# Four graph layers on 64 graphs: layer 2 projects before it aggregates

## The chip, the cores and the metric

The kernel runs on one core of one Trainium2 chip. A core has five engines with an instruction queue each: TensorE (PE in the profile; its weight loads are listed as PEld), VectorE (DVE), ScalarE (ACT), GpSimd (POOL) and SyncE (SP), which here issues all DMA transfers. The metric is the device time of one launch in microseconds; a time is the median of several runs. All data is fp32.

## What is computed

64 graphs of 256 nodes with 512 features go through four layers. Each layer normalizes x, clips it at zero to give h, computes a graph layer from h and the adjacency matrix, and adds the result to x. Layer 2, the one that the change is about, and layer 3 read:

```python
def _L2_gnn_ref(x, a, kernel):          # x is h, 256 x 512; a is 256 x 256
    t = jnp.einsum('bnm,bmf->bnf', a, x)
    out = jnp.einsum('bnf,fd->bnd', t, kernel)
    out = jax.nn.relu(out)
    mask = (jnp.sum((x != 0).astype(jnp.float32), axis=-1, keepdims=True) > 0).astype(jnp.float32)
    return out * mask

def _L3_gnn_ref(x, adj, W):
    deg = jnp.sum(adj, axis=-1, keepdims=True)
    agg = jnp.einsum('bij,bjf->bif', adj, x) / jnp.maximum(deg, EPS)
    cat = jnp.concatenate([x, agg], axis=2)
    out = jnp.einsum('bnf,of->bno', cat, W)
    return jax.nn.relu(out)

# layer l:  h = jnp.maximum(_layernorm(x, axis=-1), 0.0);  x = x + layer_l(h, adj, ...)
```

Layer 0 is an attention layer (a softmax over the nodes of `leaky_relu(Wh1 + Wh2)`, masked where the adjacency is at most 0.5, then `elu`). Layer 1 uses A + I scaled on both sides by the square root of its row sums, with a bias and a ReLU. A product A h W can be taken as (A h) W or as A (h W); the result is the same but for rounding.

## The kernel before

**Products of halves.** A product of two matrices is taken by 2 x 2 blocks with seven block products instead of eight (Winograd's form of Strassen's scheme). The left matrix is held as seven blocks A11, A12, S1, A22, S2, S4, S3 and the right one as B11, B21, B22, T1, T2, T3, T4N; S and T are sums and differences of blocks. `project` (L525) issues the seven products of one or more operand pairs into three PSUM banks, pz, pv and py. Between the four products in pz, the block there is copied out (`snap`, L555) by ACT or DVE; `add` (L561) adds the blocks in pv and py on DVE. The first three result blocks end in a tile c, or where `places` says; the last one stays in pz and is given to `last`. An operand is either `Weighted` (L488: a node tile times one of the five weight tiles wb, two matmuls to a product) or `Gathered` (L503: blocks of the adjacency aT and their sums aw times a projected tile y, one matmul to a product).

**A layer.** In layers 0, 1 and 2, `aggregate` (L464) first multiplies h by the adjacency (eight matmuls, L474, into two PSUM banks pt). This leaves the aggregate with the features along the partitions, as the projection needs it. `left_sums` (L450) copies it into the tile xw and makes S1 (L459); `more_sums` (L440) makes S2 on DVE and S3 and S4 on POOL (L446). Then `project` multiplies xw by the layer's weight, 14 matmuls, and `into_x` (L602) adds the result to xs on DVE, with the row sums (total) that the next norm needs. The first two graphs (`FIRST`) do layer 0 in another order.

Layer 3 already goes the other way. It turns h3 so that its features lie along the partitions: DVE transposes 32 x 32 blocks into the tile hb (L820), and 16 DMA transfers (L825) move the blocks to their place in hw, in runs of 128 bytes. DVE makes hw's S1 (L830), `more_sums` the rest. A first `project` (L840) multiplies hw by wb4 and leaves its blocks in the tiles y and y12 (the copies are L582 and L841, the totals L584); four differences (L848, three on DVE, one on POOL) complete y. Four sums of blocks of aT (L854 to L860, on POOL) make aw. A second `project` (L863) takes hw times wb3 and aT times y together, three matmuls to a product. Before that, aT is scaled in place by the row 1 / degree (L814), which `along` (L361) turns and spreads with a DVE transpose and two DMA transfers.

Layer 1 uses A + I, made by three POOL operations (L745, L749) in the tile ahT.

**The order.** Every instruction is entered by `op` (L219) with its engine, a planned duration, what it reads and writes, and its tiles. `Plan.place` (L72) then simulates all engines and gives each the next instruction that can start, by urgency and due time; it also gives out the buffers of each tag. The planned durations are multiplied by `STRETCH`; a product on PE is ranked as if its input came `SPARE` us later. `APART` is the distance of the graphs' due times, shortened to a part `LATE` for the last `LAST` graphs. The engines then execute their lists strictly in that order. Buffers are given by tag (L879): among them xs (7), aT (6), h (3), xw (5, for xw0 to xw2, hw and y), mva (6, for e, ahT and aw), c (3), hb (1, also used while the weights are loaded, L267 and L326).

Of the kernel before, what the change touches and what calls it, by code (L numbers as in the profile page):

```python
# [11 lines left out]
ALU = mybir.AluOpType  # L12
AX = mybir.AxisListType

P = 128
Q = 32
# [3 lines left out]
ALPHA = 0.2  # L20
NEG_INF = -9000000000000000.0
HOP = 0.25
APART = 14.0
ON_PE = 3
FIRST = 2
LAST, LATE = 4, 0.3

STRETCH = {"DVE": 1.15, "ACT": 1.1, "POOL": 1.15, "PE": 1.0, "DMA": 1.0}
SPARE = 0.3

# [119 lines left out]
def kernel(  # L152
# [39 lines left out]
    class Tiles:  # L192
# [5 lines left out]
        def declare(self, name, shape, pool=None, tag=None):  # L198
            tag = pool or tag or name
            self.tiles[name] = Buffered(shape, tag, f"{name}_{self.name}")  # L200
# [63 lines left out]
    def weight(n, w):  # L264

        me = Tiles(f"w{n}", 0.0)
        me.declare("b12", [P, FH, OH], tag="hb")  # L267
        for at, i, j in ((B11, 0, 0), (None, 0, 1), (B22, 1, 1), (B21, 1, 0)):
            block = w[i * FH * P : (i + 1) * FH * P, j * OH : (j + 1) * OH].rearrange(
                "(k p) o -> p k o", p=P  # L270
            )
            me.op("DMA", 256, lambda g, at=at, block=block: nc.sync.dma_start(  # L272
                g["b12"] if at is None else wb[n][:, at], block),
                  (), ["b12" if at is None else f"=wb{n}.{at}"])
        weight_sums(me.op, n, "b12")
        if n == 0:
            logit_weights(me)
# [43 lines left out]
    def last_weight():  # L321

        me = Tiles("w3", 0.0)
        op, declare = me.op, me.declare
        for n in range(2):
            declare(f"b12_{n}", [P, FH, OH], tag="hb")  # L326
        for c in range(O // P):
            j, o = divmod(c * P, OH)
            declare(f"w3n{c}", [P, 2 * F], tag="h")
            op("DMA", 512, lambda g, c=c: nc.sync.dma_start(  # L330
                g[f"w3n{c}"], w3[c * P : (c + 1) * P, :]), (), [f"w3n{c}"])
            for n in range(2):
                for i in range(NC):
                    pw = f"pw{c}{n}{i}"
                    declare(pw, [P, FH, P], "ps")

                    def go(g, c=c, n=n, i=i, pw=pw):
                        for k in range(FH):
                            f0 = n * F + (i * FH + k) * P
                            nc.tensor.transpose(  # L340
                                g[pw][:, k], g[f"w3n{c}"][:, f0 : f0 + P], ident
                            )

                    op("PE", 0.23, go, [f"w3n{c}", "=ident"], [pw])
                    at = (B21 if i else B11) if j == 0 else (B22 if i else None)
                    key = f"b12_{n}" if at is None else f"=wb{3 + n}.{at}"
                    op("ACT", 0.38, lambda g, n=n, at=at, o=o, pw=pw: nc.scalar.copy(
                        (g[f"b12_{n}"] if at is None else wb[3 + n][:, at])[:, :, o : o + P],
                        g[pw]), [pw], [key])
        for n in range(2):  # L350
            weight_sums(op, 3 + n, f"b12_{n}")
# [4 lines left out]
    def graph(b):  # L356
# [251 lines left out]
               reads + to_keys, to_keys + ([f"{t}.{key}"] if sums else []), urgent=urgent)  # L608

        declare("ab", [P, NC, N], tag="ab")
        declare("aT", [P, NC, N])
# [121 lines left out]
        else:  # L735
# [7 lines left out]
        declare("ahT", [P, NC, N], tag="mva")  # L743
        flat = lambda t: t.rearrange("p c n -> p (c n)")
        op("POOL", 0.75, lambda g: nc.gpsimd.tensor_copy(  # L745
            flat(g["ahT"])[:, P : 3 * P], flat(g["aT"])[:, P : 3 * P]), ["aT"], ["ahT.off"])
        for c in range(NC):
            at = slice(3 * c * P, (3 * c + 1) * P)
            op("POOL", 0.5, lambda g, at=at: nc.gpsimd.tensor_tensor(  # L749
                flat(g["ahT"])[:, at], flat(g["aT"])[:, at], ident, ALU.add),  # L750
               ["aT", "=ident"], [f"ahT.{c}"])
        aggregate("h1", "ahT", 1, ["ahT.off", "ahT.0", "ahT.1"])

        def scaled(g, i, to, block, j):
# [36 lines left out]
           ["mask.0", "mask.1"], ["mask.0", "mask.1"])  # L791


        aggregate("h2", "aT", 2)

        def masked(i, key, y, y_keys, to, to_keys, n, at, tag):
            v = f"v2{tag}"
            declare(v, [P, n], tag=f"ex{n}")
            op("ACT", 0.5 if n == 256 else 0.72, lambda g: nc.scalar.activation(
                g[v], y(g), AF.Relu, scale=g["mask"][:, i : i + 1]), y_keys + [f"mask.{i}"], [v],  # L800
               urgent="pz2" in y_keys)
            into_x(2, key, at, 0.43 if n == 256 else 0.69,
                   lambda g, kw: nc.vector.scalar_tensor_tensor(
                       to(g), g[v], 0.0, to(g), ALU.add, ALU.add, **kw), [v], to_keys)

        first, second, third = pieces(2)
        project([Weighted("xw2", 2)], 2, plain_keep, 0.38, plain_total, lambda _: masked(*first, "a"))
        masked(*second, "b")
        masked(*third, "c")
        norm(3)  # L810


        along("pr", lambda g: g["rdeg"], ["rdeg"])
        op("DVE", 0.69, lambda g: nc.vector.tensor_tensor(  # L814
            g["aT"], g["aT"], g["pr"].rearrange("p (o n) -> p o n", o=1).to_broadcast([P, NC, N]),
            ALU.mult), ["pr", "aT"], ["aT"], urgent=True)

        declare("hb", [P, NC, F])
        for c in range(NC):
            op("DVE", 0.71, lambda g, c=c: nc.vector.transpose(g["hb"][:, c, :], g["h3"][:, c, :]),  # L820
               [f"h3.{c}"], [f"hb.{c}"])
        declare("hw", [P, 7, FH, P], tag="xw")
        parts = [(a, q) for a in range(P // Q) for q in range(P // Q)]
        for a, q in parts:
            op("DMA", 32, lambda g, a=a, q=q: nc.sync.dma_start(  # L825
                g["hw"][q * Q : (q + 1) * Q, : 2 * NC].rearrange("j s k n -> j (s k) n")[
                    :, :, a * Q : (a + 1) * Q],
                g["hb"][a * Q : (a + 1) * Q].rearrange("j c (k q r) -> q j (c k) r", q=P // Q, r=Q)[q]),
               ["hb.0", "hb.1"], [f"hw.{a}{q}"], holds=0.7)
        op("DVE", 0.43, lambda g: nc.vector.tensor_tensor(  # L830
            g["hw"][:, S1], g["hw"][:, S1], g["hw"][:, A22], ALU.add),
           [f"hw.{a}{q}" for a, q in parts], [f"hw.{i}" for i in (A11, A12, A22, S1)], urgent=True)
        more_sums("hw")

        declare("y", [P, 7, OH], tag="xw")
        declare("y12", [P, OH], tag="ex256")
        places = {(0, 0): (lambda g: g["y"][:, B11], f"y.{B11}"),
                  (0, 1): (lambda g: g["y12"], "y12"),
                  (1, 1): (lambda g: g["y"][:, B22], f"y.{B22}")}
        project([Weighted("hw", 4)], 4, plain_keep, 0.38, plain_total,  # L840
                lambda pz: op("ACT", 0.38, lambda g: nc.scalar.copy(g["y"][:, B21], g[pz]),  # L841
                              [pz], [f"y.{B21}"], urgent=True), places=places)
        for eng, us, to, i, j in (("DVE", 0.43, T1, None, B11), ("POOL", 0.85, T3, B22, None),
                                  ("DVE", 0.43, T2, B22, T1), ("DVE", 0.43, T4N, B21, T2)):
            name = lambda n: "y12" if n is None else f"y.{n}"
            of = lambda g, n: g["y12"] if n is None else g["y"][:, n]
            on = nc.vector if eng == "DVE" else nc.gpsimd
            op(eng, us, lambda g, on=on, to=to, i=i, j=j: on.tensor_tensor(  # L848
                g["y"][:, to], of(g, i), of(g, j), ALU.subtract), [name(i), name(j)],
               [f"y.{to}"], urgent=True)  # L850

        declare("aw", [P, 4, P], tag="mva")
        block = lambda g, c, i: g["aT"][:, c, i * P : (i + 1) * P]
        op("POOL", 0.5, lambda g: nc.gpsimd.tensor_tensor(  # L854
            g["aw"][:, 0], block(g, 0, 1), block(g, 1, 1), ALU.add), ["aT"], [f"aw.{S1}"])
        op("POOL", 0.5, lambda g: nc.gpsimd.tensor_tensor(
            g["aw"][:, 1], g["aw"][:, 0], block(g, 0, 0), ALU.subtract),
           ["aT", f"aw.{S1}"], [f"aw.{S2}"])
        for at, to, i in ((2, S3, 1), (3, S4, 0)):
            op("POOL", 0.5, lambda g, at=at, i=i: nc.gpsimd.tensor_tensor(  # L860
                g["aw"][:, at], block(g, 1, i), g["aw"][:, 1], ALU.subtract),
               ["aT", f"aw.{S2}"], [f"aw.{to}"])
        project([Weighted("hw", 3), Gathered("aT", "aw", "y")], 3, plain_keep, 0.38, plain_total,  # L863
                lambda _: relu_add(3, *pieces(3)[0]))
        _, second, third = pieces(3)
        relu_add(3, *second)
# [10 lines left out]
    for b in range(B):  # L877
        graph(b)
    buffers = dict(  # L879
        xs=7, a_nat=1, ab=1, aT=6, h=3, mva=6, xw=5, c=3, off=1, junk=1, ex256=2, ex512=2,  # L880
        a_rows=1, a_cols=1, turned=1, row=4, pl=1, pr=1, hb=1, ps=8,
    )
    for tag in ("stats", "total", "mv", "rstd", "nb", "deg", "dh", "rdeg", "lg", "top", "den", "mask"):
        buffers[tag] = 6
# [34 lines left out]
```

## Time and profile before

| | |
|---|---|
| median of 3 runs | 2832.87 us (2832.54 to 2833.22) |
| the profiled execution | 2832.82 us, of which 2831.0 us from the first to the last instruction (the span) |
| granted clock of TensorE | 1.000 |
| DMA | 159.10 MB in 493747 packets, 424644 of them under 512 bytes; 23.9% of the 16 DMA engines' time on SP's queue |
| largest group of DMA issues | hw<-hb, 1024 of 32.0 KB each (16 per graph), 609 ns median for SP to issue one |

An entry of the profile's groups reads: line, engine, operation, output <- inputs, shape, count | busy time in us, mean ns of one | idle time of the engine in front of them, and what ended it. Buffer numbers are left out of the names, so hw0 and hw1, or y and y12, are one name. An fp32 matmul appears as two MATMUL records and two LDWEIGHTS records. Records on PE overlap: the sum of their durations is more than the time in which PE was busy.

These are some of the times of one instruction that are used later:

```
L820 DVE STREAM_TRANSPOSE hb<-h 128x512 f32<-128x512 f32 x128 | 86.2, 689
L848 DVE TENSOR_TENSOR y<-y 128x256 f32<-128x256 f32 x128 | 79.9, 625
L848 DVE TENSOR_TENSOR y<-y,y 128x256 f32<-128x256 f32 x64 | 27.7, 433
L848 POOL TENSOR_TENSOR y<-y,y 128x256 f32<-128x256 f32 x64 | 61.6, 962
L454 ACT COPY xw<-pt 128x512 f32<-128x512 f32 x192 | 112.4, 585
L457 ACT COPY xw<-pt 128x256 f32<-128x256 f32 x192 | 71.4, 372
```

### The profile page before, as it was taken

The page shows a single profiled execution, that of the slowest core. Times are in us where ns is not written, and L with a number is a line of the kernel's source. Part 1 is how long each engine was busy: PE and PEld are TensorE (multiplying, and loading weights), DVE is VectorE, ACT ScalarE, POOL GpSimd, SP SyncE. Part 2 cuts the span into 40 slices and gives each one's busy share as a digit, 9 for nine tenths or more (in the row PEclk, how much of TensorE's full clock was granted, in tenths as well). Part 3 has the DMA queues.
Part 4 walks back from the last instruction along what each step waited for, and adds up shares of the span by engine and source line. Part 5 has one row for each costly group of instructions (what it writes and reads, how often), then busy time and mean ns, then how long its engine had stood idle before and what let it go on. Part 6 is the DMA issues. An engine that isn't in the chain of part 4 may idle for free.

```text
span 2831.0 us, 42966 instructions
## 1 busy us (share of the span) xinstructions
PE 2813.3 (99%) x12999; PEld 2464.8 (87%) x12999; DVE 1911.0 (68%) x5111; ACT 1707.6 (60%) x4118; POOL 1202.9 (42%) x2333
## 2 busy tenths in 40 slices
PE   8999999999999999999999999999999999999999
PEld 5888888888888888888888888888888888888888
DVE  7776667666666766667667666676666666666654
ACT  6766666666666666666656566666665666556552
POOL 7654434344344444443443434444434344343341
PEclk9999999999999999999999999999999999999999
DMA  5123222222222222222222222222222222221112
GB/s 173 25 64 74 67 48 56 63 47 59 57 49 64 49 55 63 46 59 51 55 64 49 55 62 47 59 52 53 65 45 58 55 46 52 42 52 39 43 33 53
DMA packets 493747, 159.10 MB, mean 56 GB/s; under 512 B 424644, under 2 KB 460108, under 8 KB 493516
## 3 DMA queue, kind: packets, MB, share of 16 engines
q1 hardware_dynamic: 493516, 156.36, 23.9%
q8 instruction: 104, 1.70, 0.3%
q14 instruction: 127, 1.04, 0.1%
HBM read 89.00 MB, written 33.68 MB: 43 GB/s over the span
## 4 chain that ended last, share of the span: by engine, by line
PE 98%; POOL 0%; DVE 0%; DMA 0%; ACT 0%; issue 0%; SPq 0%; DVEq 0%; POOLq 0%
PE pz L543 43%; PE pt L474 23%; PE pv L543 21%; PE py L543 11%; PE pwa_w L311 0%; POOL wb L260 0%; DMA a_rows_w<-in_L_gnn_a_dram 0%; PE po L723 0%; ACT h L436 0%; PE pw_w L302 0%; DMA pl<-dpl 0%; PE pt L705 0%; SPq L272 0%; DMA dpl<-tpl 0%; POOL xw L446 0%
## 5 line engine op out<-in xcount | busy, mean ns | idle before, releaser
L543 PE MATMUL pz<-wb,xw 128*128 128x256 f32 x3072 | 764.2, 379 | 3.5 <-ACT wh L582 2.1
L543 PEld LDWEIGHTS pz<-wb,xw 128*128 128x128 f32 x3072 | 582.9, 190 | 85.0 <-ACT wh L582 1.9
L543 PE MATMUL pz<-wb,hw 128*128 128x256 f32 x2048 | 524.2, 379 | 0.5 <-ACT c L582 0.5
L543 PEld LDWEIGHTS pz<-wb,hw 128*128 128x128 f32 x2048 | 389.0, 190 | 53.7 <-ACT c L582 0.9
L582 ACT COPY c<-pz 128x256 f32<-128x256 f32 x570 | 208.0, 370 | 329.7 <-PE pz L543 328.7
L436 ACT ACTIVATE h<-xs,nb,rstd 128x512 f32<-128x512 f32 x512 | 398.4, 809 | 10.3 <-POOL nb L433 7.2
L543 PE MATMUL pv<-wb,xw 128*128 128x256 f32 x1536 | 394.3, 379 | 0.9 <-DVE mv L401 0.8
L446 POOL TENSOR_TENSOR xw<-xw 128x256 f32<-128x256 f32 x384 | 299.6, 800 | 164.3 <-DVE xw L442 74.1
L543 PEld LDWEIGHTS pv<-wb,xw 128*128 128x128 f32 x1536 | 291.5, 190 | 41.2 <-POOL wb L260 0.9
L584 DVE TENSOR_TENSOR c<-pv,c 128x256 f32<-128x256 f32 x380 | 160.3, 422 | 232.6 <-PE pv L543 194.7
L415 ACT ACTIVATE h<-xs,mv 128x512 f32<-128x512 f32 x384 | 276.5, 721 | 6.2 <-POOL mv L412 4.9
L543 PE MATMUL pv<-wb,hw 128*128 128x256 f32 x1024 | 262.5, 379 | 0.0
L474 PE MATMUL pt<-ahT,h 128*128 128x256 f32 x1024 | 240.9, 379 | 0.9 <-ACT h L436 0.9
L474 PE MATMUL pt<-aT,h 128*128 128x256 f32 x1024 | 236.8, 379 | 0.0
L474 PE MATMUL pt<-e,h 128*128 128x256 f32 x992 | 225.0, 379 | 0.4 <-ACT e L675 0.4
L409 POOL TENSOR_SCALAR mv<-total 128x1 f32<-128x1 f32 x192 | 111.7, 582 | 261.2 <-DVE xs L691 134.0
L454 ACT COPY xw<-pt 128x512 f32<-128x512 f32 x192 | 112.4, 585 | 178.7 <-PE pt L474 178.6
L474 PEld LDWEIGHTS pt<-ahT,h 128*128 128x128 f32 x1024 | 194.5, 190 | 28.1 <-ACT h L436 1.7
L543 PEld LDWEIGHTS pv<-wb,hw 128*128 128x128 f32 x1024 | 194.6, 190 | 26.5
L474 PEld LDWEIGHTS pt<-aT,h 128*128 128x128 f32 x1024 | 194.6, 190 | 26.4
L474 PEld LDWEIGHTS pt<-e,h 128*128 128x128 f32 x992 | 188.3, 190 | 26.4 <-ACT e L675 0.8
L459 DVE TENSOR_TENSOR xw<-pt,xw 128x256 f32<-128x256 f32 x192 | 80.2, 418 | 178.4 <-ACT xw L454 171.2
(136 smaller groups left out, 4690.6 us busy)
## 6 DMA issues: line engine op xcount, KB each, us to landing
xs<-in_x_dram SPq DMA_DIRECT2D x64, 512.0 KB
hw<-hb SPq DMA_DIRECT2D x1024, 32.0 KB
out_dram<-xs SPq DMA_DIRECT2D x64, 512.0 KB
ab<-in_adj_dram SPq DMA_DIRECT2D x512, 32.0 KB
a_nat<-in_adj_dram SPq DMA_DIRECT2D x64, 256.0 KB
pr<-dpr SPq DMA_DIRECT2D x64, 128.0 KB
pl<-dpl SPq DMA_DIRECT2D x61, 128.0 KB
w3n_w<-in_L_gnn_W_dram SPq DMA_DIRECT2D x4, 512.0 KB
```

Source lines behind the costliest of these rows:

```text
L409: op("POOL", 0.3, lambda g: nc.gpsimd.tensor_scalar(g[mv][:, 0, 1:2], g[t][:, 1:2], g[t][:, 2:3], -1.0 / F, ALU.add, ALU.mult), [f"{t}.10" ...
L415: op("ACT", 1.0, lambda g, c=c: nc.scalar.activation(g[h][:, c, :], g["xs"][:, c, :], AF.Square, bias=g[mv][:, 0, c : c + 1], accum_out=g[ ...
L436: op("ACT", 0.81, lambda g, c=c: nc.scalar.activation(g[h][:, c, :], g["xs"][:, c, :], AF.Relu, bias=g[nb][:, c : c + 1], scale=g[rs][:, c ...
L446: op("POOL", 0.85, lambda g, i=i, o=o: nc.gpsimd.tensor_tensor(g[xw][:, o], g[xw][:, i], g[xw][:, S2], ALU.subtract), put(i, S2), put(o), ...
L454: op("ACT", 0.59, lambda g: nc.scalar.copy(g[xw][:, A12 : A22 + 1 : A22 - A12].rearrange("p h k n -> p k h n"), g[hi].rearrange("p k (h n) ...
L459: op("DVE", 0.43, lambda g: nc.vector.tensor_tensor(g[xw][:, S1], g[lo][:, :, P:], g[xw][:, A22], ALU.add), [lo] + put(A22), put(S1), urge ...
L474: nc.tensor.matmul(g[pt][:, kk, :], lhsT=g[h][:, c, k * P : (k + 1) * P], rhs=g[moving][:, c, :], start=(c == 0), stop=(c == NC - 1),)
L543: nc.tensor.matmul(g[t], lhsT=o.left(g, left, k), rhs=o.right(g, right, k), start=start and n == 0, stop=n == len(parts) - 1, skip_group_c ...
L582: return "ACT", lambda g, to, block: nc.scalar.copy(to, block)
L584: plain_total = (0.43, lambda g, i, to, block: nc.vector.tensor_tensor(to, block, to, ALU.add))
```

## The change

Layer 2 takes the order of layer 3: it turns h2, projects it by wb2, and multiplies the adjacency by the result with seven products of one matmul each. The code of layer 3 for this becomes three functions with the layer as an argument. The turn now happens in h itself instead of in hb, and the tag hb is gone. Three things get an added input that holds them back until their layer begins: ahT waits for total1.0 (the end of layer 0's sum), the degree row for total2.0, and the block sums for h of their layer. Buffers and the constants of the planner change too.

```diff
-APART = 14.0
+APART = 16.0
-LAST, LATE = 4, 0.3
-STRETCH = {"DVE": 1.15, "ACT": 1.1, "POOL": 1.15, "PE": 1.0, "DMA": 1.0}
-SPARE = 0.3
+LAST, LATE = 3, 0.5
+STRETCH = {"DVE": 1.15, "ACT": 1.03, "POOL": 1.25, "PE": 1.0, "DMA": 1.0}
+SPARE = 0.5
...
-        me.declare("b12", [P, FH, OH], tag="hb")
+        me.declare("b12", [P, FH, OH], tag="ex512")
...
+        def turn(l):
+            h, hw = f"h{l}", f"hw{l}"
+            for c in (1, 0):
+                op("DVE", 0.71, lambda g, c=c: nc.vector.transpose(g[h][:, c, :], g[h][:, c, :]),
+                   [f"{h}.{c}"], [f"{h}.{c}"])
+            declare(hw, [P, 7, FH, P], tag="xw")
+            parts = [(a, q) for a in range(P // Q) for q in range(P // Q)]
+            for a, q in parts:
+                op("DMA", 32, lambda g, a=a, q=q: nc.sync.dma_start(
+                    g[hw][q * Q : (q + 1) * Q, : 2 * NC].rearrange("j s k n -> j (s k) n")[
+                        :, :, a * Q : (a + 1) * Q],
+                    g[h][a * Q : (a + 1) * Q].rearrange("j c (k q r) -> q j (c k) r", q=P // Q, r=Q)[q]),
+                   [f"{h}.0", f"{h}.1"], [f"{hw}.{a}{q}"], holds=0.67)
+            op("DVE", 0.48, lambda g: nc.vector.tensor_tensor(
+                g[hw][:, S1], g[hw][:, S1], g[hw][:, A22], ALU.add),
+               [f"{hw}.{a}{q}" for a, q in parts], [f"{hw}.{i}" for i in (A11, A12, A22, S1)], urgent=True)
+            more_sums(hw)
+
+        def neighbours(l, w):
+            y, y12 = f"y{l}", f"y12{l}"
...
+            project([Weighted(f"hw{l}", w)], f"y{l}", plain_keep, 0.38, plain_total,
+                    lambda pz: op("ACT", 0.38, lambda g: nc.scalar.copy(g[y][:, B21], g[pz]),
+                                  [pz], [f"y.{B21}"], urgent=True), places=places)
+            for eng, us, to, i, j in (("DVE", 0.48, T1, None, B11), ("POOL", 0.9, T3, B22, None),
+                                      ("DVE", 0.48, T2, B22, T1), ("DVE", 0.48, T4N, B21, T2)):
...
+        def block_sums(l, a):
+            aw = f"aw{l}"
+            declare(aw, [P, 4, P], tag="mva")
+            block = lambda g, c, i: g[a][:, c, i * P : (i + 1) * P]
+            op("POOL", 0.5, lambda g: nc.gpsimd.tensor_tensor(
+                g[aw][:, 0], block(g, 0, 1), block(g, 1, 1), ALU.add), [a, f"h{l}.0"], [f"{aw}.{S1}"])
...
-            flat(g["ahT"])[:, P : 3 * P], flat(g["aT"])[:, P : 3 * P]), ["aT"], ["ahT.off"])
+            flat(g["ahT"])[:, P : 3 * P], flat(g["aT"])[:, P : 3 * P]), ["aT", "total1.0"], ["ahT.off"])
...
-               ["aT", "=ident"], [f"ahT.{c}"])
+               ["aT", "=ident", "total1.0"], [f"ahT.{c}"])
...
-        aggregate("h2", "aT", 2)
+        turn(2)
+        neighbours(2, 2)
+        block_sums(2, "aT")
...
-        project([Weighted("xw2", 2)], 2, plain_keep, 0.38, plain_total, lambda _: masked(*first, "a"))
+        project([Gathered("aT", "aw2", "y2")], 2, plain_keep, 0.38, plain_total, lambda _: masked(*first, "a"))
...
-        along("pr", lambda g: g["rdeg"], ["rdeg"])
+        along("pr", lambda g: g["rdeg"], ["rdeg", "total2.0"])
...
-        declare("hb", [P, NC, F])
...
+        turn(3)
+        neighbours(3, 4)
+        block_sums(3, "aT")
+        project([Weighted("hw3", 3), Gathered("aT", "aw3", "y3")], 3, plain_keep, 0.38, plain_total,
                 lambda _: relu_add(3, *pieces(3)[0]))
...
-        xs=7, a_nat=1, ab=1, aT=6, h=3, mva=6, xw=5, c=3, off=1, junk=1, ex256=2, ex512=2,
-        a_rows=1, a_cols=1, turned=1, row=4, pl=1, pr=1, hb=1, ps=8,
+        xs=7, a_nat=1, ab=1, aT=6, h=5, mva=5, xw=5, c=2, off=1, junk=1, ex256=3, ex512=2,
+        a_rows=1, a_cols=1, turned=2, row=16, pl=1, pr=1, ps=8,
```

In layer 3 the durations that the planner is told change only a little (0.43 to 0.48 for the DVE sums, 0.85 to 0.9 for the one on POOL, 0.7 to 0.67 for a transfer's hold on SP's queue).

More of the change, by code (lines that the diff above doesn't have):

```diff
@@ L325, in last_weight @@
         for n in range(2):
-            declare(f"b12_{n}", [P, FH, OH], tag="hb")
+            declare(f"b12_{n}", [P, FH, OH], tag="ex512")
         for c in range(O // P):
@@ new lines, in neighbours @@
+        def neighbours(l, w):
+            y, y12 = f"y{l}", f"y12{l}"
+            declare(y, [P, 7, OH], tag="xw")
+            declare(y12, [P, OH], tag="ex256")
+            places = {(0, 0): (lambda g: g[y][:, B11], f"{y}.{B11}"),
+                      (0, 1): (lambda g: g[y12], y12),
+                      (1, 1): (lambda g: g[y][:, B22], f"{y}.{B22}")}
+            project([Weighted(f"hw{l}", w)], f"y{l}", plain_keep, 0.38, plain_total,
+                    lambda pz: op("ACT", 0.38, lambda g: nc.scalar.copy(g[y][:, B21], g[pz]),
+                                  [pz], [f"{y}.{B21}"], urgent=True), places=places)
+            for eng, us, to, i, j in (("DVE", 0.48, T1, None, B11), ("POOL", 0.9, T3, B22, None),
+                                      ("DVE", 0.48, T2, B22, T1), ("DVE", 0.48, T4N, B21, T2)):
+                name = lambda n: y12 if n is None else f"{y}.{n}"
+                of = lambda g, n: g[y12] if n is None else g[y][:, n]
+                on = nc.vector if eng == "DVE" else nc.gpsimd
+                op(eng, us, lambda g, on=on, to=to, i=i, j=j: on.tensor_tensor(
+                    g[y][:, to], of(g, i), of(g, j), ALU.subtract), [name(i), name(j)],
+                   [f"{y}.{to}"], urgent=True)
@@ new lines, in block_sums @@
+        def block_sums(l, a):
[4 more added lines that the diff above has]
+                g[aw][:, 0], block(g, 0, 1), block(g, 1, 1), ALU.add), [a, f"h{l}.0"], [f"{aw}.{S1}"])
+            op("POOL", 0.5, lambda g: nc.gpsimd.tensor_tensor(
+                g[aw][:, 1], g[aw][:, 0], block(g, 0, 0), ALU.subtract),
+               [a, f"{aw}.{S1}"], [f"{aw}.{S2}"])
+            for at, to, i in ((2, S3, 1), (3, S4, 0)):
+                op("POOL", 0.5, lambda g, at=at, i=i: nc.gpsimd.tensor_tensor(
+                    g[aw][:, at], block(g, 1, i), g[aw][:, 1], ALU.subtract),
+                   [a, f"{aw}.{S2}"], [f"{aw}.{to}"])
@@ L816, in graph @@
             ALU.mult), ["pr", "aT"], ["aT"], urgent=True)
-        declare("hb", [P, NC, F])
[L819 to L862, printed above, removed]
@@ L863, in graph @@
-        project([Weighted("hw", 3), Gathered("aT", "aw", "y")], 3, plain_keep, 0.38, plain_total,
+        turn(3)
+        neighbours(3, 4)
+        block_sums(3, "aT")
+        project([Weighted("hw3", 3), Gathered("aT", "aw3", "y3")], 3, plain_keep, 0.38, plain_total,
                 lambda _: relu_add(3, *pieces(3)[0]))
```

## The prediction

> **What bounds the kernel now.** I read the shares of busy time first, then the chain that ended last, then stretches of the span, then the groups.
>
> ```profile
> span 2831.0 us, 42966 instructions
> PE 2813.3 (99%) x12999; PEld 2464.8 (87%) x12999; DVE 1911.0 (68%) x5111; ACT 1707.6 (60%) x4118; POOL 1202.9 (42%) x2333
> ...
> PE 98%; POOL 0%; DVE 0%; DMA 0%; ACT 0%; issue 0%; SPq 0%; DVEq 0%; POOLq 0%
> ```
>
> TensorE is busy for all but 17.7 us, and the chain lies on it for 98%. Three stretches say where the 17.7 us are (columns: stretch, length, then busy time and instructions of PE, weight loads, DVE, ACT, POOL, then PE's granted clock, DMA share, GB/s):
>
> ```profile
> 20.00:80.00 60.00, 53.79 (x242) 40.79 (x241) 54.61 (x139) 45.05 (x118) 48.74 (x71) 1.00 0.47 135
> 80.00:2790.00 2710.00, 2710.00 (x12558) 2385.63 (x12557) 1835.80 (x4928) 1650.30 (x3975) 1142.73 (x2240) 1.00 0.24 53
> 2790.00:2831.00 41.00, 35.51 (x164) 30.59 (x162) 15.31 (x33) 5.50 (x15) 3.25 (x4) 0.99 0.20 56
> ```
>
> Between 80 and 2790 us PE never waits, at a granted clock of 1.00. So the time there is a count of matmul records times their pitch: 2710.00 / 12558 = 0.2158 us. (The "mean ns" of 379 is latency; records overlap.) An fp32 matmul leaves two records, 0.432 us. Until 80 us PE loses 12.2 us (6.2 of them after 20 us), at the end 5.5.
>
> **The products.** These groups give what layer 2 has now and what replaces it:
>
> ```profile
> L543 PE MATMUL pz<-wb,xw 128*128 128x256 f32 x3072 | 764.2, 379 | 3.5 <-ACT wh L582 2.1
> ...
> L474 PE MATMUL pt<-aT,h 128*128 128x256 f32 x1024 | 236.8, 379 | 0.0
> ```
> ```profile
> L543 PE MATMUL pz<-y,aT 128*128 128x256 f32 x256 | 76.1, 379 | 0.0
> L543 PE MATMUL pz<-y,aw 128*128 128x256 f32 x256 | 76.1, 379 | 0.0
> L543 PE MATMUL pv<-y,aw 128*128 128x256 f32 x256 | 76.1, 379 | 0.0
> ...
> L543 PE MATMUL py<-y,aT 128*128 128x256 f32 x128 | 38.1, 379 | 0.0
> ```
>
> Removed per graph: the aggregation, 1024 / 64 = 16 records. The projection on w2 keeps its 28 (pz 3072, pv 1536, py 768 over three layers and 64 graphs: 16 + 8 + 4); only its left side is now hw2. Added: seven products of one matmul, 14 records, as layer 3 has them now (4 + 4 + 4 + 2). Net 2 records fewer per graph, 202 to 200, with the same 128x256 moving shape. In the order of time a pair of the y products in layer 3 takes 0.43 us before the next starts, so the pitch holds. 64 x 2 x 0.2158 = **27.6 us less** on PE. PE's clock cannot add to this: it is 1.00 already.
>
> **What is added elsewhere, and its cover.** DVE per graph: two turns in place (as L820, 86.2 / 64 = 1.35), hw's S1 and S2 (0.44 + 0.43), the three differences of y (L848, 79.9 / 64 + 0.43 = 1.68), three totals into y (54.2 / 64 + 27.2 / 64 = 1.27); gone are xw's S1 and S2 (0.42 + 0.45). Net +4.3 us: from 1835.80 / 2710 x 43.6 = 29.5 us of a graph's period (202 x 0.2158 = 43.6) to 33.8 of 43.2, 78%. ACT: four more copies of 0.37, less L454 and L457 (0.59 + 0.37): +0.5, to 27.1 us, 63%. POOL: T3 (0.96) and the four block sums (L854, L856, L860: 121.2 / 64 = 1.89): +2.85, to 21.2 us, 49%. SP: 16 more issues at 0.61 us = 9.7 us; its issues of one period (1499.5 to 1542.5 us) now sum to 16.8, so 26.5, 61%. DMA: the 1024 turn transfers of 32 KB in runs of 128 bytes are 262144 of 493747 packets in a load of 23.9%; as many again, at a packet's mean cost, make 37%. None passes PE, so all of it is costed at nothing, PE's work on other graphs being the cover. Were it uncovered, a graph's chain would be longer by a turn and its sums, 1.35 + 10.4 (16 issues at the 0.65 pitch seen) + 1.6 (last issue to L830) + 0.87 + 0.73 = 15 us, and by the second step, 3.0 for seven products and 1.6 for a copy and two differences, less 6.0 of the removed aggregation and its sums (8 x 0.432 + 0.59 + 0.37 + 0.87 + 0.73): 14 us per graph, some 870 in all. Seven xs and six aT buffers let three or four graphs run at once, and the products of several interleave in the order of time.
>
> How much can a busier DVE hold PE up? The trace has both cases:
>
> ```profile
> 1990.00:2000.00 10.00, 10.00 (x48) 8.79 (x47) 9.49 (x29) 6.09 (x18) 3.76 (x6) 1.00 0.28 86
> ...
> 2580.00:2600.00 20.00, 20.00 (x95) 17.60 (x94) 15.87 (x41) 11.96 (x28) 9.08 (x18) 1.00 0.04 7
> ```
>
> Here DVE is busy for 95% and 79% with PE full; from 20 to 80 us it is at 91% and PE loses 10%, though weights and POOL are late there too. Bounds: 0 and 10% at 91%, which at 78% would be 4% (112 us) on a line from 68% with no loss. I take 0, because the long saturated stretches are nearer than the start.
>
> POOL's own risk is that it and DVE slow each other: L848's DVE differences range from 412 to 945 ns, with a mean of 625 for the two whose inputs both lie in y and 433 for the third. The 1.68 above holds that already; 0.2 more on each of the four new DVE operations between SBUF tiles (S1 and the differences) is 0.8 us per graph, 80% instead of 78%. The Trainium skill, "SBUF — State Buffer", section "Who interferes with whom", says more against the change: a DVE instruction with two SBUF inputs and a GpSimd instruction that reads SBUF lock each other out for the whole instruction. By that, all 2.85 us of the new POOL work could stop DVE: 36.7 us, 85%, and still no change of the sum unless DVE decides.
>
> **What is moved.** The three POOL operations for ahT (0.42 + 2 x 0.46 = 1.3 us) now wait for total1.0, so they run in layer 1's norm rather than whenever POOL is free (now POOL idles 89.1 us in front of them, waiting for PE to free the buffer). Queued behind them on POOL are the means and powers of norm and the sums at L446, for which ACT's h and then PE wait: at most 1.3 us late per graph, covered by other graphs' products. The degree row (DVE 0.24, SP 0.55 + 0.35, behind the 16 turn issues at worst, so 10 us late) waits for total2.0, and aT's scaling (0.68) now waits for layer 2's last product from aT rather than for the aggregation. Behind them stand layer 3's block sums (1.9 us), which PE needs only after layer 3's turn (12 us) and first projected blocks. Both take 0. Buffers: mva goes from six to five with four uses per graph instead of three; xw keeps five with six uses instead of five. SP waits for PE before a turn 57 times, 4.7 us each, and would now do so twice per graph: 26.5 + 9.4 is still below 43. None of these has gain on PE to give.
>
> **The two ends.** At the start, two buffers instead of one for b12 can save at most the 5.4 us for which POOL waited for it; DVE's 4.3 us for each of some two graphs that reach layer 2 early cost at most 9. I take +2, nearer the loss, since DVE is 91% busy there. At the end (LAST and LATE draw three graphs together instead of four, but less far) a longer chain can show up: 0 if the last graphs still interleave, 14 (above) if the last one is alone. I take +1, because up to 2790 us PE is full.
>
> Sum against the profiled execution: 2831.0 - 27.6 + 2 + 1 = 2806.4 us of span; 1.8 lie around it (2832.82 for that run), so **2808 us**. The run shown stands at the median, 2832.87. Its own range is 2800 (start -5, end 0) to 2828 (+9, +14).
>
> **The rivals.** *Snaps stand open (slower).* A pz block is copied out by ACT before the next product may use its bank. Near the end, with nothing left to fill in, it shows:
>
> ```profile
> 2822.05 0.59 PE L543 MATMUL pz<-y,aw 128*128 128x256 f32 x2
> ...
> 2822.68 0.37 ACT L582 COPY c<-pz 128x256 f32<-128x256 f32 x1 [2.22 <-PE pz L543]
> ...
> 2823.11 1.13 PE L543 MATMUL pz<-wb,hw 128*128 128x256 f32 x4 [0.46 <-ACT c L582]
> ```
>
> 0.46 us per open snap. Layer 2's new products are single matmuls of 0.43 us, half of those before, and three snaps lie among four of them: 1.38 us per graph, 88 us, if nothing fills them. It decides from 27.6 / (64 x 0.46) = 0.94 open snaps per graph. With half of them open: 2808 + 44 = 2852. Against it: five projections already have 15 snaps per graph, and PE lost nothing to them in 2710 us; for it: short products fill less, and orders come from planned costs. *DVE late (part of the gain lost).* The order of all engines is planned from costs written in the kernel. For DVE they sum to 32.8 us per graph, times a stretch of 1.15, 37.7 of 43.6; after, 37.2 x 1.15 = 42.8 of 43.2. So the plan itself may leave gaps on PE, though the operations then run faster (33.8), and SPARE leaves each product 0.5 us instead of 0.3 after its input. At 0.5% of PE's time, an eighth of the bound, 14 us: 2822. *It doesn't do what it says.* The short products may not run at 0.2158 us per record; at the 379 ns of one alone, 14 x 0.163 x 64 = 146 us more; a sixth of that makes 2832, no change. The 0.43 us of a y pair speaks against it.
>
> **How the numbers follow.** Forecast 0.64, DVE late 0.17, pitch or other loss that eats the gain 0.03, open snaps 0.16. The range, 2800 to 2830, holds the forecast and most of the second, leaving out some 0.18. A measurement of this kernel tells 0.2% (5.7 us) from no change. Faster is 0.64 and 0.14 of the second; same 0.03 and 0.03; slower 0.16.
>
> **What would show it.** PE records 12871 (12999 - 128); PE busy 2785.7 at an unchanged pitch; no wait of PE in the middle of the span; DVE near 78%, 2048 turn transfers; PE idle until 80 us some 14 us. It is wrong if PE's middle stretch has gaps put down to ACT's copies at L582 (snaps), to DVE's sums of hw2 or y2, or to POOL.

## The result and the profile after

The changed kernel takes 2808.95 us (median of 4 runs, 2807.72 to 2809.52) against 2832.7 before (4 runs); the ratio is 0.9916, 95% interval 0.9899 to 0.9933. The forecast was 2808, range 2800 to 2830.

First lines and chain of the changed kernel's page:

```profile
span 2805.9 us, 45964 instructions
PE 2787.2 (99%) x12871; PEld 2440.7 (87%) x12871; DVE 2162.8 (77%) x5623; ACT 1745.7 (62%) x4246; POOL 1415.1 (50%) x2653
...
q1 hardware_dynamic: 772044, 189.98, 31.1%
...
PE 98%; DVE 1%; ACT 0%; DMA 0%; issue 0%; POOL 0%; SPq 0%; POOLq 0%; DVEq 0%; ACTq 0%
```

PE has 128 records less and is busy for 26.1 us less; the span is 25.1 us shorter. PE is idle for 18.7 us, where it was 17.7. Three stretches of the changed kernel (columns as in the prediction):

```profile
0.00:200.00 200.00, 187.09 (x828) 152.83 (x829) 159.57 (x408) 139.15 (x360) 131.02 (x224) 0.99 0.42 102
200.00:2500.00 2300.00, 2300.00 (x10658) 2024.72 (x10657) 1789.80 (x4693) 1448.46 (x3511) 1152.51 (x2183) 1.00 0.31 68
2500.00:2806.00 306.00, 300.12 (x1389) 263.16 (x1387) 213.43 (x524) 158.13 (x377) 131.60 (x248) 1.00 0.26 54
```

And the middle of the kernel before:

```profile
200.00:2500.00 2300.00, 2300.00 (x10658) 2024.72 (x10657) 1569.76 (x4224) 1400.91 (x3375) 966.22 (x1903) 1.00 0.24 55
```

In the middle both kernels are full and pass the same 10658 records, though DVE goes from 1569.76 to 1789.80 us (68 to 78%). Each graph just needs fewer of these records. The groups of the changed kernel show which:

```profile
L543 PE MATMUL pzy<-wb,hw 128*128 128x256 f32 x2048 | 516.8, 379 | 0.6 <-ACT y L582 0.6
...
L474 PE MATMUL pt<-ahT,h 128*128 128x256 f32 x1024 | 241.0, 379 | 0.0
...
L543 PE MATMUL pz<-y,aw 128*128 128x256 f32 x512 | 152.4, 379 | 0.2 <-DVE y L647 0.2
...
L543 PE MATMUL pz<-y,aT 128*128 128x256 f32 x512 | 152.1, 379 | 0.0
```

The 1024 records pt<-aT,h are gone, and the y products have doubled (pz<-y,aT from 256 to 512). Idle time in front of the y products is 0.7 us in all (0.2 before pz<-y,aw and 0.5 before pv<-y,aw, both waiting for L647), and none of it lies between 200 and 2500 us: the short products found their fill.

### The profile page after: what moved, and what is told of

It reads as the page before. It is cut to its first block, busy times and chain, and to the rows that moved or that the text cites. A ratio compares the mean times of both kernels' runs of the same rounds, so it can differ in the third digit from the quotient of the medians.

```text
span 2805.9 us, 45964 instructions
## 1 busy us (share of the span) xinstructions
PE 2787.2 (99%) x12871; PEld 2440.7 (87%) x12871; DVE 2162.8 (77%) x5623; ACT 1745.7 (62%) x4246; POOL 1415.1 (50%) x2653
## 3 DMA queue, kind: packets, MB, share of 16 engines
q1 hardware_dynamic: 772044, 189.98, 31.1%
## 4 chain that ended last, share of the span: by engine, by line
PE 98%; DVE 1%; ACT 0%; DMA 0%; issue 0%; POOL 0%; SPq 0%; POOLq 0%; DVEq 0%; ACTq 0%
PE pz L543 31%; PE pzy L543 16%; PE pv L543 16%; PE pt L474 16%; PE pvy L543 8%; PE py L543 8%; PE pyy L543 4%; PE pwa_w L311 0%; PE po L779 0%; DMA a_rows_w<-in_L_gnn_a_dram 0%; DVE e L698 0%; DVE e L718 0%; PE pw_w L302 0%; SPq L272 0%; DVE xs L747 0%
## 5 line engine op out<-in xcount | busy, mean ns | idle before, releaser
L543 PE MATMUL pz<-wb,xw 128*128 128x256 f32 x2048 | 523.9, 379 | 2.9 <-DVE c L811 1.2
L543 PE MATMUL pzy<-wb,hw 128*128 128x256 f32 x2048 | 516.8, 379 | 0.6 <-ACT y L582 0.6
L543 PEld LDWEIGHTS pz<-wb,xw 128*128 128x128 f32 x2048 | 388.1, 190 | 58.3 <-DVE c L811 1.2
L543 PEld LDWEIGHTS pzy<-wb,hw 128*128 128x128 f32 x2048 | 389.0, 190 | 53.8 <-ACT y L582 1.0
L582 ACT COPY c<-pz 128x256 f32<-128x256 f32 x570 | 211.3, 371 | 307.6 <-PE pz L543 267.6
L446 POOL TENSOR_TENSOR hw<-hw 128x256 f32<-128x256 f32 x256 | 202.5, 810 | 198.8 <-DVE hw L442 99.8
L582 ACT COPY y<-pzy 128x256 f32<-128x256 f32 x384 | 142.0, 370 | 214.1 <-PE pzy L543 184.5
L543 PE MATMUL pvy<-wb,hw 128*128 128x256 f32 x1024 | 262.9, 379 | 0.1
L543 PE MATMUL pz<-wb,hw 128*128 128x256 f32 x1024 | 262.7, 379 | 0.0
L543 PEld LDWEIGHTS pvy<-wb,hw 128*128 128x128 f32 x1024 | 194.5, 190 | 26.9 <-issue 0.5
L543 PEld LDWEIGHTS pz<-wb,hw 128*128 128x128 f32 x1024 | 194.6, 190 | 26.4
L698 DVE SCALAR_TENSOR_TENSOR e<-h,wa 128x512 f32<-128x512 f32 x256 | 203.8, 796 | 11.8 <-ACT wa L318 3.9
```

The lines of the kernel that those rows point to most:

```text
L446: op("POOL", 0.85, lambda g, i=i, o=o: nc.gpsimd.tensor_tensor(g[xw][:, o], g[xw][:, i], g[xw][:, S2], ALU.subtract), put(i, S2), put(o), ...
L543: nc.tensor.matmul(g[t], lhsT=o.left(g, left, k), rhs=o.right(g, right, k), start=start and n == 0, stop=n == len(parts) - 1, skip_group_c ...
L582: return "ACT", lambda g, to, block: nc.scalar.copy(to, block)
L698: op("DVE", 0.77, lambda g, j=j, c=c: nc.vector.scalar_tensor_tensor(g["e"].rearrange("p c n -> p (c n)"), g["h0"][:, c, :], 1.0, wa[:, j, ...
```

## The experiments

All times are medians. The ratio is to the kernel before, run on the same chip, with its 95% interval. Where a cost against the changed kernel is given, it is the difference to its 2808.95 us, which were measured apart from these runs; the kernel before took 2832.1 to 2832.7 us beside each of them.

| kernel | us | ratio (interval) | PE records | idle of PE in 200 to 2500 us |
|---|---|---|---|---|
| before, new constants | 2838.4 | 1.0023 (1.0013 to 1.0033) | 12999 | 3.0 |
| after, old constants | 3026.5 | 1.0681 (1.0665 to 1.0697) | 12871 | 111.8 |
| after, two records back | 2842.8 | 1.0038 (1.0024 to 1.0052) | 12999 | 0 |
| after, APART 14 alone | 3086.1 | 1.0896 (1.0874 to 1.0917) | 12871 | 141.8 |
| after, the other five old | 2834.3 | 1.0007 (0.9996 to 1.0017) | 12871 | 0.1 |
| after, DVE dose | 2829.2 | 0.9988 (0.9979 to 0.9998) | 12871 | 0.5 |
| after, no guards | 2892.7 | 1.0213 (1.0192 to 1.0233) | 12871 | 43.7 |
| after, no block-sum guard | 2850.3 | 1.0062 (1.0042 to 1.0082) | 12871 | 6.9 |
| no guards, mva 7, h 4 | 2832.2 | 0.9999 (0.9988 to 1.0009) | 12871 | 0.5 |
| layer 1 too | 3134.4 | 1.1070 (1.1053 to 1.1086) | 12743 | 141.5 |
| layer 1 too, APART 17 | 2831.1 | 0.9995 (0.9985 to 1.0004) | 12743 | 10.2 |

**Is it the count of records?** One product of layer 2 is issued twice:

```diff
+                again = parts[:1] if l == 2 and bank == "z" and start else []
                 def go(g):
+                    for o, k in again:
+                        nc.tensor.matmul(g[t], lhsT=o.left(g, left, k), rhs=o.right(g, right, k),
+                                         start=True, stop=True, skip_group_check=True)
```

> The changed kernel with one product of layer 2 issued twice per graph (the first of the seven, overwritten by itself), which gives back the two records per graph and changes nothing else. Theory: 12999 records, 2809 + 27.6 = 2837 us, within 4. Rival (the changed kernel is held by DVE or by a graph's chain, with PE just covering it): less than half of that, under 2823 us.

It rose by 33.9 us to 2842.8, 2 us above the range that the theory allowed. PE's busy time rose by 31.2 us (2818.4 against 2787.2) and its idle time by 3.8 (22.5 against 18.7). 27.6 of the 31.2 are the records; the rest fits the granted clock, which is lower in this run in two places (0.66 against 0.83 from 40 to 50 us, and 0.94 from 2760 us on against 1.00). So the middle is bound by the number of records, and the two records are worth what they were priced at. The rival, under 2823 us, is out.

**The constants, with and without the change.** Two kernels exchange the six constants:

```diff
-APART = 14.0
+APART = 16.0
-LAST, LATE = 4, 0.3
+LAST, LATE = 3, 0.5
-STRETCH = {"DVE": 1.15, "ACT": 1.1, "POOL": 1.15, "PE": 1.0, "DMA": 1.0}
-SPARE = 0.3
+STRETCH = {"DVE": 1.15, "ACT": 1.03, "POOL": 1.25, "PE": 1.0, "DMA": 1.0}
+SPARE = 0.5
```

The kernel before with the lines marked +:

> The kernel before with the planner's six new constants alone (APART 16, LAST 3, LATE 0.5, ACT stretch 1.03, POOL stretch 1.25, SPARE 0.5), buffers and layers as before. Theory (the time is the count of matmul records times their pitch): 12999 records as before, so 2833 us, within 4. Rival (the gain came from a better order): 2809 to 2820 us, with less PE idle than the 17.7 us of before.

The changed kernel with the lines marked -:

> The changed kernel with the planner's six old constants (APART 14, LAST 4, LATE 0.3, ACT 1.1, POOL 1.15, SPARE 0.3), all else as changed. Theory: 12871 records and a middle that stays full, so 2809 us, within 6; the ends may move by some us. Rival (only the new constants keep PE full with DVE at 77%): PE idle in the middle stretch, 2820 us or more.

On the kernel before, the new constants cost 6.3 us, 1.4 us beyond what the theory allowed; the rival, a gain from a better order, is out. On the changed kernel the old ones cost 217.6. So the constants bring no gain of their own, but without them the change makes the kernel 6.8% slower. Here my theory fell and the rival stands. The middle with the old constants, and then PE's waits in it and around it (what waited <- for what: us in total, times, longest):

```profile
200.00:2500.00 2300.00, 2188.24 (x9884) 1860.31 (x9883) 1672.19 (x4341) 1336.93 (x3281) 1058.17 (x2036) 1.00 0.30 64
```
```profile
PE pz L543 <- DVE c L811: 55.7, 51, 2.5
PE pz L543 <- ACT c L582: 34.6, 60, 2.9
PE pzy L543 <- DMA hw<-h: 30.6, 24, 6.7
```

The waits in the first two lines are those of a rival of the prediction, snaps that stand open (L811 is layer 1's snap on DVE, L582 the others'). The third is for turn transfers that arrive late, which the prediction priced only as part of a graph's longer chain, not as a rival.

**Which constant?** First APART alone, in the changed kernel:

```diff
-APART = 16.0
+APART = 14.0
```

> The changed kernel with APART alone put back from 16 to 14 (distance of the graphs' due times), all else as changed. Of the 218 us that the six old constants cost, theory A (the distance of the due times decides how the graphs interleave, and with it whether PE's middle stays full): nearly all, 2990 us or more. Rival B (the margins decide, SPARE and the stretches: PE's input is planned too tightly): 2809 to 2820 us.

Then the changed kernel with the lines marked - of the diff before, but for APART, which stays 16:

> The other half of the last pair: APART stays at 16, and LAST, LATE, the ACT and POOL stretches and SPARE are put back. Theory A: the middle stays full, 2809 to 2825 us, what is lost lies at the ends. Rival B: 2990 us or more.

APART alone costs 277 us, more than all six together. The other five leave the middle full (2299.88 of 2300 us). They cost 25.4 us, 9 us more than theory A allowed, and it lies at the ends: until 200 us PE is busy for 181.85 us instead of 187.09, and after 2500 us it needs 331 us instead of 306.

What APART 14 does is seen on SP and PE. First, who held SP up, in the changed kernel:

```profile
SPq L621 <- DVE h L616: 324.2, 59, 11.7
SPq L621 <- PE pz L543: 270.4, 59, 9.0
SPq L372 <- DVE h L616: 45.0, 43, 2.8
```

and with APART 14:

```profile
SPq L372 <- DVE tpl L369: 503.3, 43, 14.5
SPq L621 <- PE pz L543: 218.7, 50, 7.9
```

In the changed kernel SP mostly waits in front of a turn (L621), for the turned h or a free buffer. With APART 14 it waits 43 times, 11.7 us each, in front of layer 0's row (L372), with the turns queued behind it. SP's issues in one period with APART 14:

```profile
1171.28 0.57 SPq L372 DMA_DIRECT2D dpl<-tpl  x1
1172.90 0.35 SPq L375 DMA_DIRECT2D pl<-dpl  x1
1177.95 21.05 SPq L621 DMA_DIRECT2D hw<-h  x32
```

and in the changed kernel:

```profile
1213.71 10.47 SPq L621 DMA_DIRECT2D hw<-h  x16
...
1230.59 10.39 SPq L621 DMA_DIRECT2D hw<-h  x16
...
1244.06 10.98 SPq L621 DMA_DIRECT2D hw<-h  x16
```

With APART 14 the turns of two graphs leave together, 32 transfers in 21 us, after SP stood still. One period later DVE transposes h from 1204.31 to 1205.6 us, SP waits for tpl until 1219.16, then 4.7 us more for a product on PE, and the turn starts at 1225.83. The changed kernel sends 16 at a time, 13 to 17 us apart. What PE does while the turn is under way, with APART 14:

```profile
1229.49 0.70 PE L543 MATMUL pz<-y,aw 128*128 128x256 f32 x2 [0.28 <-ACT c L582]
1230.74 0.67 PE L543 MATMUL pz<-y,aw 128*128 128x256 f32 x2 [0.55 <-ACT c L582]
1231.90 0.70 PE L543 MATMUL pz<-y,aT 128*128 128x256 f32 x2 [0.48 <-ACT c L582]
...
1237.87 1.10 PE L543 MATMUL pzy<-wb,hw 128*128 128x256 f32 x4 [0.56 <-issue]
```

The single products of layer 2 have little between them until hw arrives, and their snaps stand open. Over the whole run pz waits 148 times for ACT's snaps (70.2 us) and 101 times for L811 (43.8). That the held-up turns are what leaves the snaps open is read from such stretches; no run changes SP's order alone. Why 14 bunches the turns and 16 does not was not tried any further; in the traces some 200 us lie between aT's transpose (L676) and its scaling (L872) with 14, 180 to 191 with 16, and 144 to 147 before the change (L620, L814). The changed kernel thus has over four graphs between these two points instead of a little over three, and with 14 each stays longer still; there are six aT buffers.

**How much room has DVE?** Six reductions of a constant tile are added per graph, and the planner is told almost nothing of them:

```diff
+        for i in range(6):
+            declare(f"dose{i}", [P, 1], tag="dose")
+            op("DVE", 0.05, lambda g, i=i: nc.vector.tensor_reduce(g[f"dose{i}"], bias, AX.X, ALU.max),
+               [f"h2.{i % 2}", "=bias"], [f"dose{i}"])
         turn(2)
```

> The changed kernel with six more DVE reductions of a constant 128x512 tile per graph, results not used (0.68 us each, 4.1 us per graph, DVE from 77% to some 87%), which the planner is told cost 0.05 us each, so that the order of the other work hardly moves. Theory (DVE is covered by PE in this order with room to spare): PE still full in the middle, 2809 to 2820 us. Rival (DVE at 87% in a fixed order holds PE up): 0.5 us per graph or more, 2841 us or more.

```profile
0.00:200.00 200.00, 179.35 (x773) 143.16 (x774) 164.11 (x412) 134.35 (x346) 124.63 (x211) 0.98 0.38 95
200.00:2500.00 2300.00, 2299.46 (x10653) 2023.39 (x10652) 1923.93 (x5003) 1454.90 (x3507) 1122.23 (x2186) 1.00 0.31 68
```

In the middle DVE is busy for 84%, less than the 87% expected, and PE still passes 10653 of 10658 records, so the theory holds there up to 84%. The time lies between the two expectations, 20.2 us up: PE is 7.7 us less busy in the first 200 us and the rest is lost after 2500 us. With the pipeline full DVE has room; while it fills and empties it seems to have less, though the run does not separate the load from small shifts in the order.

**The guards.** The added inputs are taken away, all three and then the block sums' alone:

```diff
-            flat(g["ahT"])[:, P : 3 * P], flat(g["aT"])[:, P : 3 * P]), ["aT", "total1.0"], ["ahT.off"])
+            flat(g["ahT"])[:, P : 3 * P], flat(g["aT"])[:, P : 3 * P]), ["aT"], ["ahT.off"])
-               ["aT", "=ident", "total1.0"], [f"ahT.{c}"])
+               ["aT", "=ident"], [f"ahT.{c}"])
-        along("pr", lambda g: g["rdeg"], ["rdeg", "total2.0"])
+        along("pr", lambda g: g["rdeg"], ["rdeg"])
-                g[aw][:, 0], block(g, 0, 1), block(g, 1, 1), ALU.add), [a, f"h{l}.0"], [f"{aw}.{S1}"])
+                g[aw][:, 0], block(g, 0, 1), block(g, 1, 1), ALU.add), [a], [f"{aw}.{S1}"])
```

> The changed kernel without the added inputs that hold ahT, the degree row and the block sums back until their layer begins (total1.0, total2.0, h of the layer), constants and buffers as changed. Theory of the prediction (the waits give and cost nothing on PE): 2809 us, within 6. Rival (made early, these tiles hold their mva and pr buffers while other graphs wait for them; in layer 1 and 2 a graph's chain then stalls): PE idle in the middle, 2840 us or more.

The second kernel has the last pair of lines only:

> The changed kernel where only the block sums' added input (h of the layer) is taken away; ahT and the degree row keep theirs. The three together cost 84 us when taken away. Theory C (the block sums aw, made too early, hold mva buffers through a whole layer, and this is the largest part): 2835 to 2875 us. Rival D (ahT's or the degree row's guard is what matters): 2809 to 2820 us.

The prediction's theory falls: without guards it takes 83.7 us more. Without the block sums' alone it takes 41.3 more, half of that, so theory C stands against D, but not that this guard is the largest part: the other 42.4 us belong to the other two guards or to all three together, which was not separated. Of the 41.3 us only 16 are work missing in the middle (10584 of 10658 records); the rest lies at the ends. Then the buffers that the guards may stand in for:

```diff
-        xs=7, a_nat=1, ab=1, aT=6, h=5, mva=5, xw=5, c=2, off=1, junk=1, ex256=3, ex512=2,
+        xs=7, a_nat=1, ab=1, aT=6, h=4, mva=7, xw=5, c=2, off=1, junk=1, ex256=3, ex512=2,
```

> The changed kernel with no guards at all, as in the run at 2893 us, but with seven mva buffers instead of five, paid for by one h buffer (four instead of five). Theory C (the guards stand in for buffers of the tag mva): most of the 84 us comes back, 2815 to 2845 us. Rival E (without guards POOL's in-order queue is the trouble: early sums stand in front of the norms): 2880 us or more.

The middle without guards, and then without guards but with seven mva buffers:

```profile
200.00:2500.00 2300.00, 2256.26 (x10355) 1969.88 (x10354) 1763.67 (x4561) 1401.02 (x3417) 1143.76 (x2128) 0.99 0.30 66
```
```profile
200.00:2500.00 2300.00, 2299.51 (x10651) 2023.02 (x10650) 1790.82 (x4686) 1437.96 (x3499) 1175.90 (x2183) 1.00 0.31 67
```

303 records are missing in the middle without guards, 65 us of work. The largest group of PE's waits there is 16.8 us, in 4 waits, for layer 0's e, which is itself a tile of the tag mva. With two more mva buffers the middle is full again, and the time is back to 2832.2. So the guards stand in for buffers: a tile made when its input is there, but read a layer later, keeps a buffer from others. Rival E is out. The 23 us that stay lie at the ends (PE busy for 180.11 of the first 200 us), where the h buffer that paid for it may be missed; that was not separated.

**Can it go on?** Layer 1 in the same way takes 128 more records away:

```diff
-        aggregate("h1", "ahT", 1, ["ahT.off", "ahT.0", "ahT.1"])
+        AH = ["ahT.off", "ahT.0", "ahT.1"]
+        turn(1)
+        neighbours(1, 1)
+        block_sums(1, "ahT", AH)
...
-        project([Weighted("xw1", 1)], 1, scaled_keep, 0.49, scaled_total, last1, ["dh", "=bias"])
+        project([Gathered("ahT", "aw1", "y1", AH)], 1, scaled_keep, 0.49, scaled_total, last1, ["dh", "=bias"])
```

> The changed kernel with layer 1 taken in the same way as layer 2: h1 turned, projected by wb1, then seven products with A + I and its block sums. 128 records fewer again, 12743. DVE would go from 33.8 to some 38 of 42.7 us per graph (89%), POOL to some 24 (56%), SP's issues to some 36 (85%). Theory, if PE still covers it: 2809 - 27.6 = 2781 us. Rival (at 89% DVE, or SP with its waits, holds PE up): PE idle in the middle stretch, 2800 us or more.

It takes 3134.4 us, so the theory falls; PE is idle for 141.5 us in the middle, 69.3 of them for hw. Then with four other constants:

```diff
-APART = 16.0
+APART = 17.0
-STRETCH = {"DVE": 1.15, "ACT": 1.03, "POOL": 1.25, "PE": 1.0, "DMA": 1.0}
+STRETCH = {"DVE": 1.02, "ACT": 1.01, "POOL": 0.95, "PE": 1.0, "DMA": 1.0}
```

> Layer 1 taken in the new way too, as in the run at 3134 us, with APART 17 and the stretches DVE 1.02, ACT 1.01, POOL 0.95 in place of 16, 1.15, 1.03, 1.25. 12743 records, 2750 us of PE. Theory (DVE near 89% still leaves PE full in the middle if the order suits; the 3134 us were the order's): middle nearly full, 2795 to 2830 us, what is lost lies in the first 200 us and at the end. Rival (DVE's load, or SP with 40 turn and load issues more, holds PE up whatever the order): 2900 us or more.

```profile
0.00:200.00 200.00, 172.00 (x711) 133.61 (x712) 161.03 (x395) 128.16 (x321) 130.81 (x211) 0.95 0.42 96
200.00:2500.00 2300.00, 2289.77 (x10574) 2005.25 (x10573) 2049.36 (x5113) 1447.81 (x3618) 1402.77 (x2453) 1.00 0.41 80
2500.00:2830.00 330.00, 319.60 (x1461) 275.04 (x1459) 255.54 (x628) 175.08 (x438) 173.76 (x310) 1.00 0.35 69
```

303 us of the loss were the order's (which of the four constants did it was not tried): with DVE at 89% PE is 99.6% busy in the middle. The time, 2831.1, is 1 us above the range expected, and no gain over the change: against the changed kernel 117 records are missing in the first 200 us, 25 us, and 84 in the middle, 18 us. No version that was run beats the changed kernel.

## Why the prediction came out right, point by point

- **128 records of 0.2158 us, 27.6 us.** Right: 12871 records, PE busy for 2787.2 us where 2785.7 were forecast, pitch in the middle unchanged. Giving two records back took the time up by 33.9 us, the 27.6 and 6.3 more.
- **Cover by other engines.** Right in this kernel: DVE 77% of the span (78 forecast for the middle, 78 measured), ACT 62 (63), POOL 50 (49). The means of single groups moved both ways (up: DVE's xs<-exa,xs from 416 to 610 ns, POOL's xw sums from 800 to 858; down: DVE's y<-y differences from 625 to 548, POOL's y<-y,y from 962 to 895), at no cost to PE. So these means do not decide on the page's rule that the prediction weighed. DMA came out at 31.1% instead of 37: the transfers' time went from 23.9% of 2831.0 us to 31.1% of 2805.9, on 16 engines some 3140 us for 278528 more packets, 11 ns each, where I took the mean of 22.
- **The ends, +2 and +1.** PE is idle for 12.9 us in the first 200 (12.2 before) and 5.9 after 2500 us (5.5). PE is busy 1.5 us longer than forecast, which fits the 1.8 us by which eight records near the start were slower (last section). The sign of "some 14 us" idle until 80 us did not come out: it was 11.1, and 1.8 more came between 80 and 200 us.
- **What is moved: "Both take 0", "None of these has gain on PE to give".** Wrong as a reason, and hidden by the result: the guards carry 83.7 us. I asked what their waits cost, and they cost nothing; I didn't ask what the same tiles do without them, with mva cut from six to five and four uses per graph.
- **The constants, costed at a sentence.** The sum took it as given that seven xs and six aT buffers keep PE full. The runs show that this hangs on APART: 2808.95 at 16, 3086.1 at 14. The sum has no term for it, so that the cover held here is owed to constants that came with the change, not to the reasons given; in that the forecast was lucky. The share of DVE says little of this: at 71% with APART 14 the kernel loses 277 us, at 84% with the dose it loses 0.5 us in the middle.
- **Open snaps.** The rival was the right mechanism and had 0.16; it is part of what happens with APART 14. Its price was too low. From 200 to 2500 us that run passes 9606 records, 227 us of work less than a full stretch, with 275 waits of 137.8 us listed: 0.83 us per wait, of which 0.50 are listed as idle. 218 of the 275 are snaps, so this is a mean over more than snaps; taken as the price of one, an estimate, it decides from about half an open snap per graph, not from 0.94.
- **DVE late.** Not seen in the middle: after 80 us PE waits 0.7 us in all for DVE's differences of y (L647), and never for hw.

## What to carry to other kernels

Where one engine is full, price a change by its instructions on that engine; then ask what keeps it full, which here was less the other engines' shares than the order, and try the change with the old order too. A step that is made as early as its input allows takes a buffer for as long as it is early. In this static schedule the restructuring and its tuning belong together: neither of the two halves here gains, one costs 0.2% and the other 6.8%.

## What the runs showed of the hardware that was not expected

A wait of PE costs more than the idle time listed for it: the last record before it no longer overlaps the next (0.379 us instead of 0.216 from start to end of its time), and the records after it are longer. In the APART 14 lines above, a pair that takes 0.43 us in a full stretch starts 1.25 us before the next, of which 0.55 are listed.

In the changed kernel's profile the granted clock fell in one place. PE waits 3.4 us for ACT's wb (L347), and the eight po records after it take 5.39 us where the kernel before took 3.60:

```profile
44.48 5.39 PE L779 MATMUL po<-wh,e 128*128 128x512 f32 x8 [3.39 <-ACT wb L347]
```
```profile
44.83 3.60 PE L723 MATMUL po<-wh,e 128*128 128x512 f32 x8
```

The stretch from 45 to 50 us has a granted clock of 0.70 there, and 1.00 before the change. The Trainium skill, "TensorE: Matmul & The Clock Gate", section "HAM oscillation — how this bites in real kernels", warns of idle gaps of PE above some 3.4 us. In this trace the gap was 3.39 us, just under that. In other runs shorter gaps did the same, as here in the changed kernel with the other five constants old:

```profile
49.66 3.69 PE L474 MATMUL pt<-ahT,h 128*128 128x256 f32 x16 [2.14 <-POOL rstd L423]
...
68.03 5.41 PE L474 MATMUL pt<-e,h 128*128 128x256 f32 x16 [2.01 <-ACT e L731]
```

After 2.14 us the granted clock was 1.00 (50 to 52 us) and the 16 records took 3.69 us; after 2.01 us it was 0.50 (70 to 72 us) and they took 5.41. So in these runs a gap of 2 us can be enough and need not be, and the page's figure is no safe limit; what else decides is not shown.
